# Expert second product by columns for the ranks of 144 to 176 rows, and turned back one expert later

## The chip, the cores and the metric

The kernel runs on one core of a Trainium2 chip. A core has five engines that run side by side and meet at semaphores: TensorE (PE: matrix products, and transposes through an identity matrix, with its weight loads shown apart as PEld), VectorE (DVE), ScalarE (ACT), GpSimd (POOL) and SyncE (SP, which issues DMAs). In this kernel the products of TensorE go to PSUM, and ScalarE and VectorE carry them from PSUM to SBUF. The metric is the device time of one execution in microseconds: 678.12 us before, the median of 3 runs (677.0 to 678.4).

## The reference, cut to what matters

A float32 transformer layer over 2 x 1024 tokens of 256 channels: attention, then a mixture of experts with 60 experts of 176 hidden units, four experts to a token, and a shared expert of 704 units.

```python
# x: layer norm of the tokens, [2048, 256]
weights, sel = top_k(softmax(x @ gate_w.T), 4)          # each token's four experts
for e in range(60):
    gu = x @ w13[e].T                                   # first product, 2 x 176 columns
    h = silu(gu[:, :176]) * gu[:, 176:]
    sparse += cw[:, e, None] * (h @ w2[e].T)            # second product, back to 256
shared = silu(x @ se_gate.T) * (x @ se_up.T) @ se_down.T * sigmoid(x @ shared_gate.T)
out = x_in + shared + sparse
```

The change concerns `h @ w2[e].T` alone.

## The kernel before, in words

Attention and routing come first. Routing scatters every token's row to a slot of each of its four experts in DRAM (`xg`), counts the tokens of each expert, and ranks the experts by that count. `CAPS` (L37) gives each rank a fixed number of rows: 6 ranks of 208, 4 of 192, 8 of 176, 10 of 160, 8 of 144 and 24 of 128. A rank with more than 128 rows is two tiles of half as many rows each (`tile_of`, L1164): 2 x 88 for 176, 2 x 80 for 160, 2 x 72 for 144. `turn_of` (L959) spreads the sizes evenly over the 60 places of the expert loop; its last five places are 176, 144, 128, 160, 128.

The expert loop (L1225) takes one place at a time. In the order in which it is written, place k does this:

- `up` (L910): the first product of place k, twelve TensorE instructions (six float32 matmuls of two instructions each) whose moving operand is xT, as wide as the rank has rows. ScalarE (L924, L926) and VectorE (L925, L927) make h in one of three buffers `hbuf`: a [128, 2, rows] tile with the hidden units on the partitions (128 in the first half, 48 and zeros in the second) and the tokens along the free axis.
- `turned` (L1177): the rows of place k+2, which came by DMA as `xe`, are turned by TensorE transposes (L1182) and copied to xT by VectorE (L1188).
- `second` (L1191) of place k-1. VectorE works out where each row goes back to (`place`, L952 and L956, into `dst`). For each tile of rows, TensorE holds that tile of h as the stationary operand, streams the 256 columns of w2 past it, twice for the two halves of the hidden units, and leaves rows x 256 in a PSUM tile `ye`. ScalarE copies both tiles to `ys` (L1207), and GpSimd scatters each tile by an indirect DMA to `yt` in DRAM (`send_back`, L933).
- Then SP issues the load of the rows of place k+4 (`rows_of`, L1172) and of the weights of place k+7 (`bring`, L984; eight buffers `w`, 624 KB each).

In this loop the order on ACT, DVE and SP is the written one (`manual_schedule`, L1211). PE and POOL are not in that list: there the planner of the framework chooses among instructions whose inputs it expects to be there, and prefers those written earlier. The PSUM pool `ps_y` has two buffers, handed out in turn to tiles tagged `ye`; a buffer is written again only when ScalarE has copied out what was in it two tiles before. `ys`, `dst` and xT have four buffers each; a buffer of `ys` or `dst` is free once the scatter that read it has landed.

Behind the loop stand a block for experts with more tokens than their rank holds (L1278; its condition is read by every engine, and here it is not entered), and then the second half of the shared expert (L863, L885), whose TensorE work runs while SP brings `yt` back (L1301) and VectorE adds it up with the routing weights (L1303). The first of these loads waits for the last scatter.

Of the kernel before, what the change touches and what calls it, by code (L numbers as in the profile page):

```python
# [8 lines left out]
F32 = mybir.dt.float32  # L9
# [7 lines left out]
P = 128  # L17
B, T, C = 2, 1024, 256
# [4 lines left out]
CC = C // P  # L23
# [7 lines left out]
W1C = 2 * P + 64 + IB  # L31
# [4 lines left out]

CAPS = [208] * 6 + [192] * 4 + [176] * 8 + [160] * 10 + [144] * 8 + [128] * 24  # L37
CAP = max(CAPS)
SP = CAP // 2
ES = NT * P  # L40
OB = -(-(ES - min(CAPS)) // P)
# [10 lines left out]
def attention_moe_kernel(  # L52
# [15 lines left out]
    nc = tc.nc  # L68
# [3 lines left out]
    def pool(name, bufs, side="left", space=None):  # L72

        kw = {"side": side} if space is None else {"space": space}
        s = ExitStack()
        return s.enter_context(tc.tile_pool(name=name, bufs=bufs, reuse_waits="tile", **kw)), s
# [7 lines left out]
    ident = const.tile([P, P], F32, name="ident")  # L84
# [72 lines left out]

    void = pj.tile([SP, 2, XR], F32, name="void", bufs=1)
    nc.gpsimd.memset(void, 0.0)
    nc.gpsimd.memset(void[:, :, TOK : TOK + 1], NONE)  # L160
    for e in range(E):
        rows = xg[e * ES : e * ES + CAP, :].rearrange("(t p) c -> p t c", p=SP)
        nc.sync.dma_start(rows, void)
    zero = pj.tile([P, 2, C], F32, name="zero", bufs=1)
    nc.gpsimd.memset(zero, 0.0)
    for i in range(TOPK * NT // 2):
        rows = yt[2 * i * P : 2 * (i + 1) * P, :].rearrange("(t p) c -> p t c", p=P)
# [7 lines left out]
    down = const.tile([E, E], F32, name="down")  # L175
# [47 lines left out]
    start = const.tile([P, E], F32, name="start")  # L223
# [313 lines left out]
    def scores(b, qb, jp, jj, s):  # L537
        t0, s0 = qb * QB, s * P
        scs = []
        for half in range(2):  # L540
            sc = ps_sc.tile([P, 2, QB], F32, tag="sc", name="sc")
            scs.append(sc)
            for gg in range(2):
                r = 32 * (2 * half + gg)
                nc.tensor.matmul(  # L545
                    sc[:, gg, :],
                    lhsT=kT[b][r : r + 32, jj, s0 : s0 + P],
                    rhs=qT[b][r : r + 32, jp, t0 : t0 + QB],
                    start=True,
                    stop=True,  # L550
                )
        es = []
        exps.clear()
        i = b * TPB + s
        for sc in scs:


            ex = att.tile([P, 2, QB], F32, tag="ex", bufs=4, name="ex")
            exps.append(
                nc.scalar.activation(ex, sc, AF.Exp, scale=rqk[:, 1, i : i + 1] if b == 0 else 1.0)  # L560
            )
            es.append(ex)
        return es
# [367 lines left out]
    def send_back(y, at):  # L931

        s = nc.gpsimd.indirect_dma_start(  # L933
            out=yt[:, :],
            out_offset=bass.IndirectOffsetOnAxis(ap=at, axis=0),
            in_=y,
            in_offset=None,
            bounds_check=TOPK * NT * P - 1,
            oob_is_err=False,
        )  # L940

        if scattered:
            tc.declare_no_dep(s.ins, group="back", reason="rows of their own")
        tc.add_to_no_dep_group("back", s.ins)
        scattered.append(s)

    def place(dst, rows, me):

        n = rows.shape[0]
        k0 = small.tile([n, 1], F32, tag="k0", name="k0")  # L950
        hit = small.tile([n, TOPK], F32, tag="wh", name="wh")
        nc.vector.scalar_tensor_tensor(  # L952
            hit, rows[:, SLT : SLT + TOPK], me, kplace[0:n, :], ALU.is_equal, ALU.mult,
            accum_out=k0,
        )
        nc.vector.tensor_add(dst, k0, rows[:, TOK : TOK + 1])  # L956
# [12 lines left out]
    def expert_at(r):  # L969

        if r not in nos:
            nos[r] = nc.values_load(
                byrank[0:1, r : r + 1],
                engines=(mybir.EngineType.SP,),
                min_val=0,
# [4 lines left out]
    def bring(k):  # L980

        no = expert_at(turn_of[k])
        w = wpool.tile([P, CC * W1C + 2 * C], F32, tag="w", name=f"w{k}")
        nc.sync.dma_start(w, wexp[bass.ds(no, 1)].rearrange("o p c -> p (o c)"))  # L984
        ws.append(w)
# [10 lines left out]
    with tc.manual_schedule(engines={mybir.EngineType.PE}), ExitStack() as both:  # L996
# [34 lines left out]
        ahead = scores(*order[0])  # L1031
        for r, (b, qb, jp, jj, s) in enumerate(order):
# [22 lines left out]
            if r + 1 < R:  # L1055
                ahead = scores(*order[r + 1])
# [10 lines left out]
            for g in range(NKV):  # L1067
                nc.tensor.matmul(  # L1068
                    av[32 * g : 32 * g + 32, :],
                    lhsT=vaug[:, b * TPB + s, g, H * jj : H * jj + 32],  # L1070
                    rhs=es[g // 2][:, g % 2, :],
                    start=s == 0,
                    stop=s == TPB - 1,
# [33 lines left out]
        h = RB // 2  # L1107
# [21 lines left out]
        sp_s = ExitStack()  # L1129
        sp_s.enter_context(tc.manual_schedule(engines={mybir.EngineType.SP}))  # L1130
        blocks = range(NT * P // FB)
# [23 lines left out]
        eh, eh_s = pool("eh", 1, "right")  # L1155
        hbuf = [eh.tile([P, 2, CAP], F32, name=f"hbuf{i}") for i in range(3)]
        for h in hbuf:
            nc.gpsimd.memset(h, 0.0)
        ew, ew_s = pool("ework", 4, "right")
        ps_x, ps_x_s = pool("ps_x", 2, space=PSUM)  # L1160
        ps_gu, ps_gu_s = pool("ps_gu", 2, space=PSUM)
        ps_y, ps_y_s = pool("ps_y", 2, space=PSUM)

        def tile_of(cap):  # L1164

            return (cap // 2, 2) if cap > P else (cap, 1)

        def rows_of(r):
            rows, n = tile_of(CAPS[r])
            no = expert_at(r)  # L1170
            xe = ew.tile([P, 2, XR], F32, tag="xe", bufs=XA + 3, name=f"xe{r}")[0:rows, 0:n, :]
            nc.sync.dma_start(  # L1172
                xe, xg[bass.ds(no * ES, CAPS[r]), :].rearrange("(t p) c -> p t c", p=rows)
            )
            return xe

        def turned(r, xe):  # L1177
            rows, n = tile_of(CAPS[r])
            tp = ps_x.tile([P, CC, CAP], F32, tag="tpe", name=f"tpe{r}")[:, :, 0 : CAPS[r]]
            for t in range(n):  # L1180
                for c in range(CC):
                    nc.tensor.transpose(  # L1182
                        tp[:, c, t * rows : (t + 1) * rows],
                        xe[:, t, c * P : (c + 1) * P],
                        ident[0:rows, 0:rows],
                    )
            xT = ew.tile([P, CC, CAP], F32, tag="xT", name=f"xT{r}")[:, :, 0 : CAPS[r]]
            nc.vector.tensor_copy(xT, tp)  # L1188
            return xT

        def second(r, w, h, xe):  # L1191
            rows, n = tile_of(CAPS[r])
            dst = ew.tile([P, 2], I32, tag="dst", name=f"dst{r}")[0:rows, :]
            for t in range(n):
                place(dst[:, t : t + 1], xe[:, t, :], slotid[0:rows, r, t : t + 1])
            po = ps_y.tile([P, 2, C], F32, tag="ye", name=f"ye{r}")[0:rows, 0:n, :]
            ys = ew.tile([P, 2, C], F32, tag="ys", name=f"ys{r}")[0:rows, 0:n, :]
            for t in range(n):
                for k in range(2):
                    nc.tensor.matmul(  # L1200
                        po[:, t, :],
                        lhsT=h[:, k, t * rows : (t + 1) * rows],
                        rhs=w[:, CC * W1C + k * C : CC * W1C + (k + 1) * C],
                        start=k == 0,
                        stop=k == 1,
                    )
            nc.scalar.copy(ys, po)  # L1207
            for t in range(n):
                send_back(ys[:, t, :], dst[:, t : t + 1])

        with tc.manual_schedule(  # L1211
            engines={mybir.EngineType.Activation, mybir.EngineType.DVE, mybir.EngineType.SP}
        ):
            xes = {}
            xTs = {}

            for k in range(XA):
                xes[k] = rows_of(turn_of[k])
            with tc.issue_after(added[-1].ins):
                xTs[0] = turned(turn_of[0], xes[0])  # L1220
            xTs[1] = turned(turn_of[1], xes[1])


            ahead = None
            for k, r in enumerate(turn_of):  # L1225
                h = hbuf[k % 3]
                up(xTs.pop(k), ws[k], h, CAPS[r], ps_gu, f"{r}")
                last = (r, ws[k], h, xes.pop(k))
                if k + 2 < E:
                    xTs[k + 2] = turned(turn_of[k + 2], xes[k + 2])  # L1230
                if ahead is not None:
                    second(*ahead)
                ahead = last

                if k + XA < E:
                    xes[k + XA] = rows_of(turn_of[k + XA])
                if 1 <= k and WA + k - 1 < E:
                    bring(WA + k - 1)
            second(*ahead)


    def over_block(e, j, c0, w):
# [35 lines left out]
    with tc.If(most > 0):  # L1278
        with tc.For_i(0, E) as e:
            n_e = nc.values_load(nblk[0:1, bass.ds(e, 1)], min_val=0, max_val=OB)  # L1280
            with tc.If(n_e > 0):
                w = wpool.tile([P, CC * W1C + 2 * C], F32, tag="w", name="w_o")
                nc.sync.dma_start(w, wexp[bass.ds(e, 1)].rearrange("o p c -> p (o c)"))
                c0 = nc.values_load(
                    cap0[0:1, bass.ds(e, 1)], min_val=min(CAPS), max_val=CAP
                )
# [106 lines left out]
```

## Time and profile before

| | |
|---|---|
| median of 3 runs | 678.12 us (677.0 to 678.4) |
| the profiled execution | 678.74 us |
| its span, first to last instruction | 676.9 us |
| TensorE busy, granted clock | 663.9 us (98%), 1.00 |
| before the expert loop | 0 to 419 us |
| expert loop on TensorE | 419 to about 613.2 us |
| shared expert's second half, output | 614.5 to 676.9 us |
| VectorE, ScalarE, GpSimd in 419 to 614 us | 88.8, 65.0 and 90.5 us busy of 195 |

The span is the profiled execution from its first to its last instruction; 1.8 us of its time lie outside. Busy times of TensorE are of pipelined instructions: one that is recorded as 379 ns long may be followed by the next after 216 ns, so what an instruction costs on a full TensorE is read from the starts of a row of them, not from its duration. A group "x8" of a timeline is eight instructions in a row, and eight times their spacing is the distance from its start to the start of the next group.

### The profile page before, as it was taken

What the parts mean: (1) busy time and instruction counts of PE and PEld (TensorE: products, weight loads), DVE (VectorE), ACT (ScalarE), POOL (GpSimd) and SP (SyncE); (2) the same over time, 40 slices, a digit from 0 to 9 for tenths busy, and PEclk for the clock granted to TensorE, in tenths of its full rate; (3) what the DMA queues carried; (4) which work ended last, traced back from release to release, by engine and by line L of the source; (5) the groups of instructions that cost most, each with busy time, mean ns of one, the idle gap of its engine ahead of it and who ended that gap; (6) DMA issues with size and microseconds to landing.
All of it is one profiled execution on the core that took longest, in us unless ns stands there. A gap on an engine that the chain in (4) does not pass through costs nothing. (4 is left out here: it accounts for less than half of the span.)

```text
span 676.9 us, 12425 instructions
## 1 busy us (share of the span) xinstructions
PE 663.9 (98%) x4156; PEld 375.9 (56%) x4157; DVE 361.7 (53%) x1404; ACT 355.7 (53%) x503; POOL 185.7 (27%) x250
## 2 busy tenths in 40 slices
PE   8999999999999999999999998999999999999997
PEld 7432332442224223233235477898998989885466
DVE  5653755427154376556657755444444434543984
ACT  3678778768986787877862400333333333332210
POOL 4020020011000034533135451444444454543000
PEclk9999999999999999999999999999999999999999
DMA  8999930002100011211011084799989899933951
GB/s 274 294 285 298 333 124 1 1 1 92 42 1 1 0 43 42 75 51 50 9 51 66 34 317 163 252 292 296 298 284 307 286 287 293 299 90 113 309 178 48
DMA packets 64275, 106.33 MB, mean 157 GB/s; under 512 B 7417, under 2 KB 51209, under 8 KB 64210
## 3 DMA queue, kind: packets, MB, share of 16 engines
q1 hardware_dynamic: 55010, 86.57, 39.6%
q0 software_dynamic: 7680, 17.32, 7.4%
q10 hardware_dynamic: 1520, 1.64, 0.7%
q8 instruction: 33, 0.54, 0.3%
q14 instruction: 32, 0.26, 0.1%
HBM read 64.13 MB, written 42.45 MB: 157 GB/s over the span
## 5 line engine op out<-in xcount | busy, mean ns | idle before, releaser
L545 PE MATMUL sc<-qT,kT 32*128 32x512 f32 x1024 | 160.3, 639 | 0.8 <-DVE vaug L335 0.5
L560 ACT ACTIVATE ex<-sc,rqk 128x1024 f32<-128x1024 f32 x128 | 134.2, 1111 | 36.8 <-PE sc L545 35.1
L1068 PE MATMUL av<-ex,vaug 128*32 128x512 f32 x1024 | 137.3, 604 | 2.6 <-DVE den L586 1.8
L560 ACT ACTIVATE ex<-sc 128x1024 f32<-128x1024 f32 x128 | 124.1, 1022 | 28.2 <-PE sc L545 24.6
L933 POOL DMA_INDIRECT yt<-ys,dst x96 | 92.8, 966 | 115.2 <-ACT ys L1207 67.5
L545 PEld LDWEIGHTS sc<-qT,kT 32*128 32x128 f32 x1024 | 52.7, 183 | 109.1 <-issue 67.5
L1200 PE MATMUL ye<-w,hbuf 128*128 128x256 f32 (+5 forms) x384 | 93.3, 381 | 0.0
L739 POOL DMA_INDIRECT xg<-xs,idx x64 | 63.3, 989 | 100.7 <-DVE idx L734 73.5
L863 PE MATMUL sg<-x2T,ws_sb 128*128 128x512 f32 x176 | 78.1, 596 | 1.2 <-ACTq L1278 1.2
L917 PE MATMUL gua<-xT,w 128*128 128x128 f32 (+5 forms) x480 | 73.2, 295 | 0.5 <-DVE xT L1188 0.5
L917 PEld LDWEIGHTS gua<-xT,w 128*128 128x128 f32 x480 | 70.1, 191 | 4.8 <-issue 0.6
L1207 ACT COPY ys<-ye 128x256 f32<-128x256 f32 (+5 forms) x60 | 29.9, 499 | 73.0 <-PE ye L1200 47.4
L1200 PEld LDWEIGHTS ye<-w,hbuf 128*128 128x128 f32 (+5 forms) x384 | 58.9, 164 | 14.5
L1068 PEld LDWEIGHTS av<-ex,vaug 128*32 128x32 f32 x1024 | 20.4, 107 | 79.0 <-issue 66.1
L925 DVE TENSOR_TENSOR hbuf<-hbuf,gua 128x128 f32<-128x128 f32 (+5 forms) x60 | 18.9, 315 | 85.0 <-ACT hbuf L924 45.9
L863 PEld LDWEIGHTS sg<-x2T,ws_sb 128*128 128x128 f32 x176 | 32.6, 190 | 38.9 <-issue 35.5
L924 ACT ACTIVATE hbuf<-gua 128x128 f32<-128x128 f32 (+5 forms) x60 | 17.9, 299 | 64.7 <-PE gua L917 41.8
L506 POOL TENSOR_TENSOR t<-u,rope_sb 128x128 f32<-128x128 f32 x24 | 12.4, 545 | 129.5 <-DVE u L492 129.5
L873 ACT ACTIVATE hs<-sg 128x512 f32<-128x512 f32 (+1 forms) x24 | 14.3, 596 | 59.0 <-PE sg L863 56.7
L885 PE MATMUL so<-ws_sb,hs 128*128 128x256 f32 x192 | 42.5, 381 | 1.5 <-DVE acc L893 1.5
L917 PE MATMUL gub<-xT,w 128*112 128x128 f32 (+5 forms) x240 | 41.2, 294 | 0.0
L885 PEld LDWEIGHTS so<-ws_sb,hs 128*128 128x128 f32 x192 | 36.2, 190 | 8.2 <-DVE acc L893 2.2
(184 smaller groups left out, 663.1 us busy)
## 6 DMA issues: line engine op xcount, KB each, us to landing
w<-in_wexp_dram SPq DMA_DIRECT2D x60, 624.0 KB
xg<-void SPq DMA_DIRECT2D x60, 221.0 KB
yt<-zero SPq DMA_DIRECT2D x32, 256.0 KB
got<-yt SPq DMA_DIRECT2D x16, 512.0 KB
xe<-xg SPq DMA_DIRECT2D x24, 136.0 KB
xe<-xg SPq DMA_DIRECT2D x10, 170.0 KB
yt<-ys,dst POOLq DMA_INDIRECT x96
xe<-xg SPq DMA_DIRECT2D x8, 187.0 KB
```

What stands on the lines that cost most here:

```text
L545: nc.tensor.matmul(sc[:, gg, :], lhsT=kT[b][r : r + 32, jj, s0 : s0 + P], rhs=qT[b][r : r + 32, jp, t0 : t0 + QB], start=True, stop=True,)
L560: nc.scalar.activation(ex, sc, AF.Exp, scale=rqk[:, 1, i : i + 1] if b == 0 else 1.0)
L739: s = nc.gpsimd.indirect_dma_start(out=xg[:, :], out_offset=bass.IndirectOffsetOnAxis(ap=at_, axis=0), in_=xs[:, i, :], in_offset=None, bo ...
L863: nc.tensor.matmul(p, lhsT=ws1_sb[:, c, c0 : c0 + P], rhs=x2T[:, c, n * FB : (n + 1) * FB], start=c == 0, stop=c == CC - 1,)
L885: nc.tensor.matmul(po, lhsT=hs[:, m, t * P : (t + 1) * P], rhs=ws2_sb[:, m, :], start=m == 0, stop=m == NC2 - 1,)
L917: nc.tensor.matmul(ps[part][0:m, 0:n], lhsT=w[:, c * W1C + c0 : c * W1C + c0 + m], rhs=xT[:, c, 0:n], start=c == 0, stop=c == CC - 1,)
L924: nc.scalar.activation(h[:, 0, 0:n], ps["ga"][:, 0:n], AF.Silu)
L925: nc.vector.tensor_mul(h[:, 0, 0:n], h[:, 0, 0:n], ps["ua"][:, 0:n])
L933: s = nc.gpsimd.indirect_dma_start(out=yt[:, :], out_offset=bass.IndirectOffsetOnAxis(ap=at, axis=0), in_=y, in_offset=None, bounds_check= ...
L1068: nc.tensor.matmul(av[32 * g : 32 * g + 32, :], lhsT=vaug[:, b * TPB + s, g, H * jj : H * jj + 32], rhs=es[g // 2][:, g % 2, :], start=s == 0,
L1200: nc.tensor.matmul(po[:, t, :], lhsT=h[:, k, t * rows : (t + 1) * rows], rhs=w[:, CC * W1C + k * C : CC * W1C + (k + 1) * C], start=k == 0 ...
L1207: nc.scalar.copy(ys, po)
```

## The change

For the 26 ranks of 144, 160 and 176 rows the second product is made the other way round. The stationary operand is a 128 x 128 block of w2, the moving operand is h with only as many columns as the rank has rows, and the product comes out as columns: 128 channels on the partitions, the tokens along the free axis, two such blocks in one `ye` tile. ScalarE copies that to a new SBUF tile `yT` (two buffers). One expert later, behind the next expert's second product, TensorE turns the four blocks of `yT` back to rows with transposes against the identity into another tile tagged `ye`, ScalarE copies that to `ys`, and the two scatters follow. The ranks of 208, 192 and 128 rows stay as they were.

```diff
+BY_COLUMNS = 176
@@ def second(r, w, h, xe):
-            po = ps_y.tile([P, 2, C], F32, tag="ye", name=f"ye{r}")[0:rows, 0:n, :]
-            ys = ew.tile([P, 2, C], F32, tag="ys", name=f"ys{r}")[0:rows, 0:n, :]
-            for t in range(n):
+            po = ps_y.tile([P, 2, C], F32, tag="ye", name=f"ye{r}")
+            down = w[:, CC * W1C :].rearrange("p (k c) -> p k c", k=2)
+
+            def send(po):
+                ys = ew.tile([P, 2, C], F32, tag="ys", name=f"ys{r}")[0:rows, 0:n, :]
+                nc.scalar.copy(ys, po[0:rows, 0:n, :])
+                for t in range(n):
+                    send_back(ys[:, t, :], dst[:, t : t + 1])
+
+            if not P < CAPS[r] <= BY_COLUMNS:
...
+                send(po)
+                return None
+            for c in range(CC):
                 for k in range(2):
                     nc.tensor.matmul(
-                        po[:, t, :],
-                        lhsT=h[:, k, t * rows : (t + 1) * rows],
-                        rhs=w[:, CC * W1C + k * C : CC * W1C + (k + 1) * C],
+                        po[:, c, 0 : CAPS[r]],
+                        lhsT=down[:, k, c * P : (c + 1) * P],
+                        rhs=h[:, k, 0 : CAPS[r]],
                         start=k == 0,
                         stop=k == 1,
                     )
-            nc.scalar.copy(ys, po)
-            for t in range(n):
-                send_back(ys[:, t, :], dst[:, t : t + 1])
+            yT = ew.tile([P, CC, CAP], F32, tag="yT", bufs=2, name=f"yT{r}")[:, :, 0 : CAPS[r]]
+            nc.scalar.copy(yT, po[:, :, 0 : CAPS[r]])
+
+            def turn():
+                tp = ps_y.tile([P, 2, C], F32, tag="ye", name=f"yr{r}")
+                for t in range(n):
+                    for c in range(CC):
+                        nc.tensor.transpose(
+                            tp[0:rows, t, c * P : (c + 1) * P],
+                            yT[:, c, t * rows : (t + 1) * rows],
+                            ident,
+                        )
+                send(tp)
+
+            return turn
@@ the expert loop
-            ahead = None
+            ahead = left = None
...
+                turn, left = left, None
                 if ahead is not None:
-                    second(*ahead)
+                    left = second(*ahead)
+                if turn is not None:
+                    turn()
...
-            second(*ahead)
+            for turn in (left, second(*ahead)):
+                if turn is not None:
+                    turn()
```

More of the change, by code (lines that the diff above doesn't have):

```diff
@@ L1195, in second @@
                 place(dst[:, t : t + 1], xe[:, t, :], slotid[0:rows, r, t : t + 1])
-            po = ps_y.tile([P, 2, C], F32, tag="ye", name=f"ye{r}")[0:rows, 0:n, :]
-            ys = ew.tile([P, 2, C], F32, tag="ys", name=f"ys{r}")[0:rows, 0:n, :]
-            for t in range(n):
+            po = ps_y.tile([P, 2, C], F32, tag="ye", name=f"ye{r}")
[7 more added lines that the diff above has]
+                for t in range(n):
+                    for k in range(2):
+                        nc.tensor.matmul(
+                            po[0:rows, t, :],
+                            lhsT=h[:, k, t * rows : (t + 1) * rows],
+                            rhs=down[:, k, :],
+                            start=k == 0,
+                            stop=k == 1,
+                        )
+                send(po)
+                return None
+            for c in range(CC):
                 for k in range(2):
                     nc.tensor.matmul(
-                        po[:, t, :],
-                        lhsT=h[:, k, t * rows : (t + 1) * rows],
-                        rhs=w[:, CC * W1C + k * C : CC * W1C + (k + 1) * C],
+                        po[:, c, 0 : CAPS[r]],
+                        lhsT=down[:, k, c * P : (c + 1) * P],
+                        rhs=h[:, k, 0 : CAPS[r]],
                         start=k == 0,
@@ L1206, in second @@
                     )
-            nc.scalar.copy(ys, po)
-            for t in range(n):
-                send_back(ys[:, t, :], dst[:, t : t + 1])
+            yT = ew.tile([P, CC, CAP], F32, tag="yT", bufs=2, name=f"yT{r}")[:, :, 0 : CAPS[r]]
+            nc.scalar.copy(yT, po[:, :, 0 : CAPS[r]])
+            def turn():
+                tp = ps_y.tile([P, 2, C], F32, tag="ye", name=f"yr{r}")
+                for t in range(n):
+                    for c in range(CC):
[3 more added lines that the diff above has]
+                            ident,
+                        )
+                send(tp)
+            return turn
         with tc.manual_schedule(
```

## The prediction

> **What bounds the kernel now.** I read the page first: its first part, then its chain.
>
> ```profile
> PE 663.9 (98%) x4156; PEld 375.9 (56%) x4157; DVE 361.7 (53%) x1404; ACT 355.7 (53%) x503; POOL 185.7 (27%) x250
> ...
> PE sg L863 6%; PE so L885 3%; DVE acc L893 0%
> ```
>
> The chain that ended last is TensorE alone, and it goes back only to 614.5 us, where TensorE waited for the end of the expert block. The change lies before that, so the stage has to be read for itself: busy time in a window cut inside the expert loop.
>
> ```profile
> 430.00:590.00 160.00, 160.00 (x1064) 144.00 (x1063) 73.34 (x387) 53.37 (x148) 76.89 (x80) 1.00 0.91 293
> ```
>
> In order: length, PE, PEld, DVE, ACT, POOL, clock, DMA share, GB/s. TensorE has no gap in 160 us, VectorE is busy 46%, ScalarE 33%, GpSimd 48%. DMA is the only rival, at 0.91. In the waits of the stage (419 to 614 us) TensorE's own idle time before the matmuls comes to about 1 us. So a TensorE nanosecond saved in this loop is one saved in the end, as long as DMA and the buffers keep up.
>
> Its price comes from the starts in the timeline of TensorE.
>
> ```profile
> 500.07 0.76 PE L917 MATMUL gub<-xT,w 128*112 128x176 f32 x4
> 500.67 0.38 PE L1182 MATMUL tpe<-ident,xe 128*128 128x128 f32 x2
> 500.89 1.89 PE L1200 MATMUL ye<-w,hbuf 128*104 128x256 f32 x8
> 502.62 1.14 PE L917 MATMUL gua<-xT,w 128*128 128x144 f32 x8
> 503.60 0.65 PE L917 MATMUL gub<-xT,w 128*112 128x144 f32 x4
> 504.09 0.44 PE L1182 MATMUL tpe<-ident,xe 80*128 80x80 f32 x4
> 504.37 1.90 PE L1200 MATMUL ye<-w,hbuf 128*88 128x256 f32 x8
> 506.10 1.05 PE L917 MATMUL gua<-xT,w 128*128 128x128 f32 x8
> ...
> 507.43 0.38 PE L1182 MATMUL tpe<-ident,xe 128*128 128x128 f32 x2
> 507.65 1.89 PE L1200 MATMUL ye<-w,hbuf 128*72 128x256 f32 x8
> 509.37 1.25 PE L917 MATMUL gua<-xT,w 128*128 128x160 f32 x8
> 510.46 0.71 PE L917 MATMUL gub<-xT,w 128*112 128x160 f32 x4
> ```
>
> Start to start, a float32 instruction with 256 moving columns takes (506.10 - 504.37) / 8 = 0.216 us, the same for 104, 88 or 72 stationary columns: half-filled weights save nothing, which is what the change is after. 176 columns take 0.60 / 4 = 0.150, 160 take 1.09 / 8 = 0.136, 144 take 0.98 / 8 = 0.1225. A transpose of 128 columns takes 0.22 / 2 = 0.11, and it is one instruction where a matmul is two.
>
> **What the Trainium skill says.** "Perfetto Trace Analysis", section "Identifying the Most-Contended Engine", says that matmul busy time is no measure of how full TensorE is, and to look at LDWEIGHTS busy time. Here that is 144 of 160 us, 90%, so both agree. "TensorE: Matmul & The Clock Gate", section "LDWEIGHTS (loading the stationary operand)", has a load take its stationary columns divided by 1.2 in ns: an estimate of 107 ns for 128. The trace fits: `gua` with 128 stationary and 128 moving columns runs at 0.89 / 8 = 0.111 us (506.10 to the `gub` group at 506.99), while 144 moving columns, at 0.1225, show nothing of the load. The full blocks that the change loads therefore stay hidden behind 144 columns or more. The same page, section "Part 4: PE-mode transpose", warns of about 275 ns for a transpose in context and of a copy behind it; the records do say 273 ns, but the spacing of 0.11 us is what a full TensorE pays. "Perfetto Trace Analysis", section "DMA Instruction — SWDGE (GPSIMD)", says that a scatter's record ends with its descriptors, not its data; so I took landings from the trace's semaphore records.
>
> **The change part by part, on TensorE.** Removed per expert: eight instructions x 0.216 = 1.73 us. Added: two column blocks x two halves x two instructions = eight at the rank's own width, and four transposes x 0.11 = 0.44.
> - 176 rows: 8 x 0.150 + 0.44 = 1.64, saves 0.09; eight such ranks, 0.7 us.
> - 160 rows: 8 x 0.136 + 0.44 = 1.53, saves 0.20; ten ranks, 2.0 us.
> - 144 rows: 8 x 0.1225 + 0.44 = 1.42, saves 0.31; eight ranks, 2.5 us.
>
> The sum is 5.2 us. No transpose against the full identity with 88, 80 or 72 stationary columns is in the trace; from below its cost is 0.11 (the stream), from above 0.15 if the narrow float32 load showed, which would take 26 x 4 x 0.04 = 4.2 us back. I take 0.11, since existing transposes with 128 stationary columns run at that. Each turn adds waits to TensorE's queue; the existing sixty of L917 (51 ns each) leave no gap in the starts, so nothing, and 26 x 0.05 = 1.3 us if none hides. A gain beyond 5.2 has no source in the loop but the rounding of these rows, 0.2 us.
>
> **ScalarE.** Added: 26 copies of 2 x rows elements. Between the copies of 256 (373 ns) and 512 elements (582 ns) that is 0.45, 0.425 and 0.40 us: 8 x 0.45 + 10 x 0.425 + 8 x 0.40 = 11 us on 65 of 195. It hides under TensorE. The silu of the next expert queues behind both copies, and VectorE's product behind that. The cover is the distance between h finished and h used: for the expert whose L927 ends at 605.65 us, `second` starts at 608.44, 2.8 us later.
>
> **PSUM buffers.** Two `ye` tiles per expert instead of one, in two buffers. By the written order the buffer of a product held the tile two back, which is copied before `up` and `turned` (1.6 us or more) are through; the turn's buffer likewise. `yT` is copied a whole expert (about 3.2 us) before its turn. No wait.
>
> **Scatters, `ys` and `dst`.** 52 scatters start one expert later. Queued on GpSimd behind the next expert's, they can bunch to four in a row, at 0.97 + 0.30 us each. The reuse of `dst` comes nearest:
>
> ```profile
> L956 DVEq EVENT_SEMAPHORE  x56: 21/50/50, 436.8 to 611.9; - x56
> L1207 ACT COPY ys<-ye x60: 372/581/586, 423.8 to 613.7; 128x256 f32<-128x256 f32 x24, 80x512 f32<-80x512 f32 x10, 88x512 f32<-88x512 f32 x8, 72x512 f32<-72x512 f32 x8
> ```
>
> At most 50 ns: this wait is free now. Setting the scatters' landings (2.1 to 6.5 us after their issue) against the `dst` that reuses the buffer four experts on, I find 1.3 to 9.4 us to spare, mostly 5 to 8; `ys` has 2.6 us or more. Less 3.2 us for the column ranks, about four places fall to zero or to -2 us, more with bunching. VectorE then waits a microsecond or two; behind it queue the next expert's two products and xT copy. VectorE idles 106 of 195 us, 1.8 per expert, and h has its 2.8: TensorE stands still only when a wait passes about 4.5 us. I count nothing.
>
> **SP and DMA.** No DMA is added. SP's weight load waits for the end of the product that frees `w`, which comes earlier. The same bytes in 2.7% less time ask for 0.93 of the engines instead of 0.91; weights land 13 to 16 us ahead of use almost throughout, rows 4 to 7. Nothing.
>
> **The end of the loop.** The place before the last has 160 rows, so its turn comes last: the copy that TensorE's next stage waits for is 0.58 instead of 0.37 us, plus 0.2. The last three scatters may all come behind the block at L1278, landing about 1.3 us later. The gathers then start later; VectorE there is up to 1.3 us late already, and with two buffers per product TensorE feels it from about 4 us. Nothing.
>
> **Sum.** -5.2 + 0.2 + 0.1 for the waits = -4.9 us. The profiled execution of 678.74 us (span 676.9) becomes 673.8 (672.0). It was 0.6 above the median, so against that: 678.12 - 4.9 = 673.2 us.
>
> **Rivals.** *Half of it is eaten* (gain 1.5 to 4, 674.1 to 676.6): narrow transposes at 0.15 us, visible queue waits, or DMA near its limit delaying rows. For it speaks the DMA share of 0.91; against it, that TensorE never waited for a row or weight in 160 us. *DMA takes over*, no measurable change: if 293 GB/s were all that this mix of packets can get, the loop would keep its length, 678 us; slices at 319 and 341 GB/s in the same window speak against. *TensorE waits for the turn*, slower: PE's order is not written by hand here, and if the planner set each turn behind its own product, TensorE would stand about 0.2 + 0.43 + 0.2 us for the copy each time. That is 26 x 0.83 = 21.6 less 4.9: about 695 us. It decides from a wait of 0.19 us a turn, where 26 of them are the gain. Against it: TensorE followed the written order in every expert of the trace before, and the planner takes what is ready first. That the change does not do what it says I exclude: the shapes are in the diff.
>
> **Chances.** The forecast 0.73 (own range 672.2 to 674.2), half eaten 0.11, DMA takes over 0.05, slower by the turn or a like wait 0.11. About 0.2% (1.4 us) is what a measurement of this kernel can tell from no change. So faster 0.84, same 0.05, slower 0.11. The range 671.8 to 676.8 takes in the first two and a spread of 0.1% between runs.
>
> **What would show it.** Right: inside the loop TensorE still without gaps; product rows at 128 x 176, 160 and 144 spaced 0.150, 0.136 and 0.1225; turns spaced 0.11; the shared half starting near 609.6 us. ScalarE's busy time up by 11 us. Wrong: idle time before the turn, released by ScalarE; `dst` waits of over 4 us on DVE's queue with TensorE idle behind them; turns spaced over 0.13.

## The result, and the profile after

The changed kernel took 672.55 us (median of 4 runs, 671.39 to 672.97) against 678.26 us before (677.0 to 678.5): a ratio of 0.9915, 95% interval 0.9900 to 0.9929. Forecast were 673.2 us and a range of 671.8 to 676.8. The experiments show that this holds on some chips and not on others. First comes what the profile says.

The page after, its first part and its chain:

```profile
PE 658.8 (98%) x4260; PEld 383.2 (57%) x4261; DVE 361.6 (54%) x1404; ACT 367.1 (55%) x529; POOL 185.9 (28%) x250
...
PE sg L864 6%; PE so L886 3%; DVE acc L894 0%
```

TensorE has 104 instructions more and is busy for 5.1 us less; ScalarE is busy for 11.4 us more. The chain is still TensorE's and starts behind the loop, so the loop is read for itself again: first busy time in the same window, then TensorE's timeline where a product by columns and a turn stand.

```profile
430.00:590.00 160.00, 160.00 (x1175) 153.19 (x1175) 75.20 (x393) 64.16 (x172) 80.42 (x84) 1.00 0.94 300
```

```profile
500.49 1.40 PE L1223 MATMUL ye<-hbuf,w 128*128 128x176 f32 x8
501.73 1.05 PE L918 MATMUL gua<-xT,w 128*128 128x128 f32 x8
502.62 0.60 PE L918 MATMUL gub<-xT,w 128*112 128x128 f32 x4
503.06 0.38 PE L1183 MATMUL tpe<-ident,xe 128*128 128x128 f32 x2
503.28 1.15 PE L1223 MATMUL ye<-hbuf,w 128*128 128x144 f32 x8
504.26 0.60 PE L1237 MATMUL yr<-ident,yT 128*88 128x128 f32 x4
504.69 0.57 PE L918 MATMUL gua<-xT,w 128*128 128x160 f32 x3
```

TensorE still has no gap in 160 us, with weight loads at 96% and DMA at 0.94. From starts: eight column products of 176 take 501.73 - 500.49 = 1.24 us, which is 0.155 each with the step to the next group, and 0.149 among themselves. Eight of 144 take 0.98, or 0.1225 each. A turn of four takes 0.43, with 0.109 from one start to the next, although 88, 80 or 72 columns are held and not 128.

Two costs that the prediction named: the reuse of `dst` on VectorE (the line's instructions, with durations least/median/most in ns, and what its engine sat idle for), and then the copies on ScalarE.

```profile
L957 DVEq EVENT_SEMAPHORE  x56: 21/50/50, 433.8 to 605.1; - x56
...
  DMA yt<-ys,dst: 0.3, 1
```

```profile
L1231 ACT COPY yT<-ye x26: 399/426/453, 424.9 to 605.1; 128x320 f32<-128x320 f32 x10, 128x352 f32<-128x352 f32 x8, 128x288 f32<-128x288 f32 x8
```

One wait of 0.3 us for a scatter in the whole loop, and 26 copies of the predicted length.

Stage by stage, the two profiles differ by 7.3 us of span: 2.0 ahead of the loop (its first product starts at 417.02, not 419.01), 4.96 in the loop from its first product to its last instruction (194.00 to 189.04), 0.38 from there to the shared half, nothing behind. The 2.0 us are not the change's: where both kernels were profiled on one chip (below, six places ahead), the loop begins at 417.63 and 417.25. It begins at 418.4 to 419.1 us in every profile with late increments (the next part says what these are) and at 416.9 to 417.6 in every other, so these two first profiles are of two kinds, and their 7.3 us are not the change's alone.

### The profile page after: what moved, and what is told of

It is laid out like the page before. It is cut to its first block, busy times and chain, and to the rows that moved or that the text cites. A ratio compares the mean times of both kernels' runs of the same rounds, so it can differ in the third digit from the quotient of the medians.

```text
span 669.6 us, 12632 instructions
## 1 busy us (share of the span) xinstructions
PE 658.8 (98%) x4260; PEld 383.2 (57%) x4261; DVE 361.6 (54%) x1404; ACT 367.1 (55%) x529; POOL 185.9 (28%) x250
## 5 line engine op out<-in xcount | busy, mean ns | idle before, releaser
L918 PEld LDWEIGHTS gua<-xT,w 128*128 128x128 f32 x480 | 67.5, 191 | 1.7 <-issue 0.5
L1212 PE MATMUL ye<-w,hbuf 128*128 128x256 f32 (+2 forms) x176 | 44.3, 383 | 0.0
L1205 ACT COPY ys<-ye 128x256 f32<-128x256 f32 (+2 forms) x34 | 14.8, 435 | 38.0 <-PE ye L1212 38.0
L918 PEld LDWEIGHTS gub<-xT,w 128*112 128x112 f32 x240 | 34.2, 177 | 0.0
```

The lines of the kernel that those rows point to most:

```text
L918: nc.tensor.matmul(ps[part][0:m, 0:n], lhsT=w[:, c * W1C + c0 : c * W1C + c0 + m], rhs=xT[:, c, 0:n], start=c == 0, stop=c == CC - 1,)
L1205: nc.scalar.copy(ys, po[0:rows, 0:n, :])
L1212: nc.tensor.matmul(po[0:rows, t, :], lhsT=h[:, k, t * rows : (t + 1) * rows], rhs=down[:, k, :], start=k == 0, stop=k == 1,)
```

## The experiments

Three things are worked out for every profile. *TensorE's own pace:* the spacings fit 0.833 ns per moving column plus 2.5 ns, and 0.11 us for 128 columns; what the starts exceed this by, summed over the loop, is its **excess**, and most of it is waiting where it is large. *The changed work itself:* for each of the 26 ranks, the time from the first start of its second product to the next start behind it, and its turn where it has one; their sum is **second**. *Late increments:* TensorE tells the other engines that a product is done by raising a semaphore by one. For each matmul in 420 to 612 us that does so, the time is taken from its recorded end to the next recorded update of that semaphore; the increment is **late** if this is over 0.3 us (the ends are modelled, but where none is late all lie at 0.014 us).

| kernel | chip | late / all | loop us | excess | second |
|---|---|---|---|---|---|
| before (first profile) | not told | 106/258 | 194.00 | 1.50 | 44.96 |
| before again | 3 | 97/257 | 195.63 | 3.12 | 44.95 |
| before, rows six ahead | 14 | 0/259 | 193.73 | 1.23 | 44.96 |
| after (first profile) | not told | 0/286 | 189.04 | 1.70 | 40.04 |
| after again | 3 | 114/282 | 198.07 | 10.72 | 40.10 |
| after, third | 14 | 0/286 | 191.18 | 3.83 | 40.04 |
| after, rows six ahead | 14 | 0/286 | 189.01 | 1.67 | 40.04 |
| the same, third | 0 | 115/287 | 190.78 | 3.45 | 40.11 |
| last rank by rows | 12 | 114/286 | 189.65 | 2.24 | 40.28 |
| 144 alone | 3 | 101/266 | 195.50 | 5.47 | 42.53 |
| turn at once | 3 | 88/265 | 209.25 | 22.00 | 60.38, with 26 waits in it |

The third column marks a kind of profile more than it counts: the traces with late increments also lack records of updates (after again has 645 for TensorE's 692 increments of the whole run, and 879 for VectorE's 1,020; the others lack almost none). That the signals are late shows without these records. From the recorded end of a product to the start of the ScalarE or VectorE instruction that takes it up, no step is over 0.5 us in any profile without late increments. In the others there are 43 of 238 (before), 47 of 238 (before again), 61 of 246 (144 alone), 18 of 264 (turn at once), 101 and 90 of 264 (after again; rows six ahead, third) and 88 of 263 (last rank by rows). ScalarE's signals do not share this: where VectorE is free, its product starts within 0.034 us of the end of ScalarE's silu, in every profile.

### Both kernels again, the turn without its delay, one size alone (chip 3)

Both kernels unchanged:

> The kernel before, unchanged. In its first profile TensorE reached the expert loop at 419.0 us, in the profile of the changed kernel at 417.0, with the same instructions ahead of it; VectorE had stood 3.7 us before the third sum behind the shared expert's first half, with the releaser given as remote. Theory (chance): that wait comes and goes from run to run; the loop starts anywhere from 416.8 to 419, and the loop itself takes 194.2 us again. Rival (systematic): the wait is part of the kernel before, and the loop starts at 419.0 within 0.3 us.

> The changed kernel, unchanged, for a narrower interval. Theory (TensorE's time in the loop, 5.1 us by the two profiles, and 0.3 us at its end): ratio 0.9920, 5.4 us. Rival (the 2 us ahead of the loop belong to the change as well): 7.3 us, ratio 0.9892.

The turn behind its own product instead of one expert later:

```diff
-                turn, left = left, None
                 if ahead is not None:
-                    left = second(*ahead)
-                if turn is not None:
-                    turn()
+                    turn = second(*ahead)
+                    if turn is not None:
+                        turn()
```

> The turn behind its own product instead of one expert later. Theory: TensorE then stands for the copy each time, 0.2 + 0.43 + 0.2 us, 26 times: 21.6 us on top of the changed kernel, about 694 us, slower than before. Rival (the planner of TensorE's order fills the gap with the next expert's first product): 673 us, no more than 1 us above the changed kernel.

Only the eight ranks of 144 rows by columns:

```diff
-BY_COLUMNS = 176
+BY_COLUMNS = 144
```

> Columns for the eight ranks of 144 rows alone. Theory (terms of the sum add up): 2.5 us less than the kernel before, 675.7 us, ratio 0.9963. Rival (the gain comes from something the pieces share, such as the scatters that start later or the weights that come free sooner): in proportion to the ranks, 8 of 26, 1.7 us or less, ratio 0.9975.

| | us (median) | ratio to before, 95% |
|---|---|---|
| before, beside | 678.95 (19 runs) | |
| before again | 680.16 (1 run) | |
| after again | 682.63 (6 runs) | 1.0052 (1.0037 to 1.0068) |
| turn at once | 693.63 (4 runs) | 1.0213 (1.0197 to 1.0229) |
| 144 alone | 679.52 (12 runs) | 1.0003 (0.9995 to 1.0012) |

**Before again** began its loop at 418.60 us, outside the 0.3 us of the rival, and took 195.63 us for it and not 194.2, because of two waits for rows.

**Turn at once** did as forecast. TensorE's waits in the loop:

```profile
PE yr L1237 <- ACT yT L1231: 8.9, 15, 0.9
PE yr L1237 <- issue: 6.3, 11, 0.8
```

All 26 turns wait; by the starts they lose 19.5 us, 0.75 each, where the rival had 0.83. In the changed kernel TensorE kept the written order, so the rival was never in play, but its price was right.

**After again** is the surprise: slower than before by 0.5%, with the code that had been faster. The last column of the first table shows that second products and turns took 4.85 us less here as well, and in 144 alone 2.4 us less. What came in was waiting: 10.7 us of excess against 3.1 in before again. TensorE's waits in the loop of after again:

```profile
PE tpe L1183 <- issue: 2.2, 3, 1.2
PE tpe L1183 <- DMA xe<-xg: 2.1, 3, 1.6
PE yr L1237 <- ACT yT L1231: 2.1, 1, 2.1
```

By the starts, six waits in front of the transposes of rows make 5.35 us, the last turn 2.29, and two second products whose h came late 0.82; before again has two waits for rows, 1.74. Why the rows are late is to be read on SyncE. Its waits in the loop, first of after (first profile), then of after again:

```profile
SPq L985 <- PE ye L1212: 40.0, 29, 4.0
SPq L985 <- PE ye L1223: 25.1, 22, 1.7
```

```profile
SPq L985 <- PE tpe L1183: 22.4, 7, 4.0
SPq L985 <- PE ye L1212: 15.9, 9, 5.4
SPq L985 <- PE ye L1223: 14.2, 12, 3.3
SPq L985 <- PE gub L918: 5.8, 4, 2.4
```

The weight load (L985) waits for the second product that frees its buffer, and for nothing else. In the first list it is let go by exactly these products. In the second it is let go in 11 cases by `tpe` or `gub`, which free no weights: there the product was done before, and its signal came later. One place of it, TensorE, ScalarE and SyncE:

```profile
462.76 0.87 PE L918 MATMUL gub<-xT,w 128*112 128x208 f32 x4
463.47 0.38 PE L1183 MATMUL tpe<-ident,xe 128*128 128x128 f32 x2
463.68 1.03 PE L1212 MATMUL ye<-w,hbuf 128*128 128x256 f32 x4
```

```profile
464.43 0.34 ACT L925 ACTIVATE hbuf<-gua 128x208 f32<-128x208 f32 x1 [2.30 <-PE ye L1212]
...
467.46 0.37 ACT L1205 COPY ys<-ye 128x256 f32<-128x256 f32 x1 [1.95 <-PE tpe L1183]
```

```profile
467.41 0.34 SPq L985 DMA_DIRECT2D w<-in_wexp_dram  x1
468.34 0.33 SPq L1173 DMA_DIRECT2D xe<-xg  x1
```

The matmuls of `ye` end at 463.68 + 1.03 = 464.71, but their copy starts at 467.46 and the weight load that they free goes out at 467.41: 2.7 us late, together. The silu of `gua`, whose matmuls had ended by 462.93, starts at 464.43. The rows behind that weight load on SyncE's queue are asked for at 468.34, 4.9 us ahead of their use where the kernel before has 7.2 at the median, and TensorE stands for them at 473.2 (0.49 us by the starts).

Of the six waits for rows, one more (1.75 us, at 557.0) is of this kind, behind a weight load 2.8 us late. The other four, 3.11 us together, are not: these rows were asked for 7.2 to 9.0 us ahead, as early as ever, and took 6.3 to 7.7 us from the ask to their last packet, where the median is 4.6 here and 4.7 in after (6.1 at most). The last of them, on SyncE and on TensorE:

```profile
505.95 0.34 SPq L985 DMA_DIRECT2D w<-in_wexp_dram  x1
507.72 0.34 SPq L985 DMA_DIRECT2D w<-in_wexp_dram  x1
510.43 0.34 SPq L985 DMA_DIRECT2D w<-in_wexp_dram  x1
511.38 0.00 SPq L1173 DMA_DIRECT2D xe<-xg  x1
520.40 0.47 PE L1183 MATMUL tpe<-ident,xe 72*128 72x72 f32 x4 [1.20 <-issue]
```

The first weight load is 1.2 us late behind its product, the next two 0.5 and 0.03, so three of 624 KB go out within 4.5 us; in after the same three take 5.7. The two waits at 489 and 492 us stand behind such a bunch as well (4.3 us against 5.8). So a late signal can delay rows in two ways: through the ask, or through a crowd of loads in the DMA queues. The second way is read from these times and was not tested by itself.

From the rows' last packet to their use there were 2.5 us at the median in after (least 1.1) and 1.9 in after again (least 0.6). Where TensorE stood for rows, this step took 0.6 to 1.3 us in after again and up to 2.4 in other profiles, so little of the 2.5 is to spare.

**144 alone** met neither number. Its second products and turns took 2.4 us less, and 5.47 us of excess ate it: between the other two, as are its late hand-overs. Seven waits make 3.65 us of it, three for rows (1.80) and four in front of second products (1.85).

The shared half behind the loop was longer, too: 65.3 us in after again, 62.35 in every other profile of the two kernels. The slice of the granted clock on its page has an 8:

```profile
PEclk9999999999999999999999999999999999998999
```

From 616.70 us on TensorE ran at half clock for 6.83 us. Just before, it had stood 2.1 us for the last turn; another 0.9 us, for the next block, fell into the slow stretch itself:

```profile
612.62 1.39 PE L1212 MATMUL ye<-w,hbuf 128*128 128x256 f32 x4
616.14 0.63 PE L1237 MATMUL yr<-ident,yT 128*80 128x128 f32 x4 [2.12 <-ACT yT L1231]
617.65 1.22 PE L864 MATMUL sg<-x2T,ws_sb 128*128 128x512 f32 x1 [0.89 <-ACTq L1318]
```

The Trainium skill, "TensorE: Matmul & The Clock Gate", section "Part 1: The HAM clock gate (the "warmup" mystery)", has the clock go to half after an idle window of about 3.4 us, on a free-running grid. 6.83 us is two such windows; but in the 3.4 us before the drop TensorE was idle for 2.1 and not for all, so here less than a whole idle window went with it. All six runs of after again had a clock of 0.994 or 0.997. The others on chip 3, which have no turn behind the last product, had 0.999 or 1.0, all 12 of 144 alone and all four of turn at once among them. That speaks for the last turn as what the clock fell on.

So the difference of the two profiles on chip 3, +4.8 us of span, is: second products and turns -4.85, the rest of the loop (waits) +7.3, the clock +2.9, the step at the end of the loop -0.4, the start -0.2. Of the waits, 3.6 us are for rows and 2.3 for the last turn. Rows are thus about a third of the 10.2 us that came in, and the last turn with the clock is half.

**The theory then:** some chips hand on TensorE's increments late; this delays SyncE, which asks late for the rows, whose slack is small. **Rivals:** DMA itself is at its limit; the increments cost through h, PSUM and the last turn rather than through the rows; or that job was an odd one.

### The chip, and the rows asked for earlier (chip 14)

The changed kernel once more, and both kernels with two more places of lead for the rows (nine `xe` buffers instead of seven):

```diff
-XA = 4
+XA = 6
```

and the changed kernel without most weight loads, so that most experts multiply by another's weights:

```diff
+        if k >= WA:
+            ws.append(ws[k - WA])
+            return
         no = expert_at(turn_of[k])
```

> The changed kernel once more, to see whether its time goes by the load and the chip. In the profile of the changed kernel that came with the result (672.55 us) none of TensorE's 286 recorded semaphore increments in the expert loop reached its recorded update over 0.3 us after the instruction's end; in the repeat on another day (682.63 us) 114 of 282 did, and in the kernel before 106 of 258. Theory (the loss comes with late increments: they hold up SyncE, which then asks for the rows late): if under 10 of them are late, 671 to 674 us; if some 100 are late, 680 to 684 us and 6 to 11 us of waits of TensorE in the loop. Rival (the repeat was an odd one): some 100 late and still 671 to 675 us.

> The changed kernel with the rows of an expert asked for six places ahead, not four, so that SyncE may be two experts (6.3 us) late with them. Theory: where increments come late, the waits in front of the transposes of rows (6.2 us in six of them in the profile of 682.9 us span) go, and with them the half-clock stretch behind the loop mostly: 674 to 677 us, against 680 to 684 of the changed kernel in the same job; where increments come on time, within 1 us of the changed kernel, 672 to 673.5. Rival (DMA at its limit delays the rows themselves): the same waits, time within 1.5 us of the changed kernel. Rival (late increments cost through other waits, of h, PSUM or the turn): under 2 us gained.

> The kernel before with the same six places, as the control. Theory: it had 1.5 to 3.1 us over TensorE's own pace in the loop, two waits for rows of 1.7 us in one profile and none in the other, so it gains 0 to 2 us: ratio 0.997 to 1.000; and the change is then worth 4 to 6 us at six places, on any chip. Rival (six places help both alike because DMA works more evenly): it gains as much as the changed kernel does.

> The changed kernel without the weight loads of the places from the ninth on: those places use the weights of the place eight before, so their output is not the product with their own weights. It takes 52 x 624 KB from the loop. Theory (TensorE's increments come late because the completions of so many DMA packets crowd the semaphores): under 15 of some 280 late, no waits for rows, loop 187 to 189 us, 671 to 674 us. Rival (they are late for a cause in the chip or the load that has nothing to do with DMA): 80 to 120 late as in the changed kernel of the same job, if that has them. If that one has none, this run tells nothing on it.

(The 6.2 us of row waits in the second text should read 5.35.)

| | us (median) | ratio to before, 95% |
|---|---|---|
| before, beside | 677.01 (15 runs) | |
| after, third | 671.76 (4 runs) | 0.9920 (0.9904 to 0.9937) |
| after, rows six ahead | 671.65 (4 runs) | 0.9920 (0.9904 to 0.9937) |
| before, rows six ahead | 676.90 (12 runs) | 0.9993 (0.9984 to 1.0002) |
| after without weight loads | 671.02 (1 run) | |

No increment is late on this chip, in either kernel, and the change is worth 5.25 us with and without the longer lead. The rows are tight even here: in the profile of after, third (its slowest run, 674.21 us) TensorE waits for them, and with six places it does not (slack 6.7 us at the least).

```profile
PE tpe L1183 <- DMA xe<-xg: 2.0, 3, 1.5
```

Without 52 of the 60 weight loads the loop takes 189.01 us, as with them at six places: with that lead, crowded DMA costs nothing here. With four places it did, in after, third: no signal was late and the rows were asked for 7.7 and 8.6 us ahead, but they took 6.2 us to their last packet, where the median is 4.5, and 2.0 without the weight loads. So the rival of DMA at its limit has a part. On late increments that run says nothing, as its text foresaw.

### A chip with late increments again

Rows six ahead was run twice more, to meet such a chip:

> The changed kernel with the rows asked for six places ahead, once more, for a chip whose increments come late. If some 100 of 286 increments of TensorE come over 0.3 us late, as on chip 3: theory (late increments hold up SyncE and so the rows) 674 to 677 us, waits in front of the transposes of rows under 1 us in sum, ratio to the kernel before 0.994 to 0.998, where the changed kernel had 1.005 on chip 3; rival (late increments cost through h, the turn and the half clock behind the loop) 680 to 683 us, ratio 1.002 to 1.006. If under 10 are late, as on chip 14: 671.65 us again, and nothing is told apart.

Chip 4: none late, 671.75 us, before 677.79, ratio 0.9908 (0.9891 to 0.9924).

> The same kernel, changed and with the rows asked for six places ahead, on whatever chip comes, since chips 14 and 4 had no late increments. On a chip with some 100 late increments of 286: theory (they hold up SyncE and so the rows) ratio to the kernel before 0.994 to 0.998 and under 1 us of waits in front of the transposes of rows; rival (they cost through h, the turn and the half clock) ratio 1.002 to 1.006, as the changed kernel on chip 3. On a chip with under 10 late: 671 to 672.5 us, and only the share of such chips is learned.

Chip 0: 115 of 287 late. 678.11 us (16 runs, 675.93 to 680.43) against 679.30: ratio 0.9977 (0.9962 to 0.9992). TensorE's waits from 417 to 608 us:

```profile
PE gua L918 <- DVE xT L1189: 0.5, 1, 0.5
PE yr L1237 <- ACT yT L1231: 0.4, 1, 0.4
```

As many late increments as on chip 3, late hand-overs as well (90 against 101), and no wait for rows, with rows that took up to 7.2 us to their last packet. The ratio lies in the theory's range. The changed kernel with four places was not run on this chip, so what the lead is worth is read across two chips. The rival of other waits has a part as well. Seven of the 16 runs had a clock of 1.0, and took 675.93 to 676.73 us (median 676.27); nine had 0.994 to 0.997, and 677.63 to 680.43 (median 679.61). In the profile, of a run at 1.0, the last turn waits 1.15 us by the starts. It has one product of 0.86 us to hide the copy that it waits for, since no first product follows it.

So the last rank by columns (place 58, 160 rows) was made as before:

```diff
-XA = 4
+XA = 6
...
-            if not P < CAPS[r] <= BY_COLUMNS:
+            if not P < CAPS[r] <= BY_COLUMNS or r == turn_of[E - 2]:
```

> Changed, rows asked for six places ahead, and the last rank by columns (place 58, 160 rows) made as before, so that no turn stands at the end of the loop with only one product of 0.86 us as its cover. On a chip with some 100 late increments: theory (the last turn waits 1.2 to 2.3 us there for a late copy, TensorE then stands again for the next block, and the clock is halved for one or two windows behind it, as in nine of the sixteen executions on chip 0): clock 1.00 or 0.999 in every execution, 675.5 to 677 us, ratio to the kernel before 0.994 to 0.997, where it was 0.9977 with the last turn. Rival (the half clock comes from waits all over the loop): clock 0.994 to 0.997 in half of the executions again, ratio 0.997 to 0.999. On a chip with under 10 late: 671.5 to 672.2 us, the turn saved (0.44 us) against the product at the rows' price (0.64 us) and the longer last copy; nothing told apart.

Chip 12: 114 of 286 late. 676.00 us (5 runs) against 679.21: ratio 0.9959 (0.9945 to 0.9973). Four runs had 1.0 and took 675.68 to 676.53; one had 0.997 and took 677.65. So one run in five had half clock for a while where the theory said none, against nine in sixteen with the last turn. With so few runs, on different chips and with intervals of the ratio that overlap, this does not show what leaving out the last turn is worth; that it does not end the half clock altogether is shown. In its profile TensorE still stands 2.28 us for the next block, at full clock.

The last run asked whether dense DMA is needed for late increments:

> The changed kernel without the weight loads of the places from the ninth on (those places multiply by the weights of the place eight before, so their output is another), once more, since chip 14 had no late increments with or without them. Chips 3, 0 and 12 had 114, 115 and 114 late increments of some 285, nearly all from 400 us on, where DMA is dense. On such a chip, theory (it takes dense DMA as well): under 30 late in the loop, no waits of TensorE for rows, span 669 to 672 us. Rival (they are late whatever DMA does): 80 to 120 late. On a chip like 14 and 4: none late, 669 us, and this stays open.

It came to chip 14 again: none late, 671.27 us. Open, as its text says.

## Why the prediction was right, and where it was not

The forecast holds where TensorE's signals come on time (672.55 us; 671.76 on chip 14). That the first measurement met such a case was luck: on chip 3 the same code took 682.63 us, outside the range.

**TensorE's terms: right.** Forecast -5.2 us; second products and turns took 44.96 us before and 40.04 after, -4.92, and 40.10 even on chip 3. By size: -0.59 for 176 rows (forecast 0.7), -1.91 for 160 (2.0), -2.43 for 144 (2.5), and the last is the same with 144 alone. What is missing is mostly the first step of each product by columns, which is longer than those behind it (0.177 us against 0.149 at 176 columns). The upper bound of 0.15 us for narrow turns is out; they take 0.109.

**ScalarE, PSUM, `dst`: right.** ScalarE was busy 75.7 us in the loop of 189 instead of 65.0 in 195. TensorE waited for no `ye` buffer in the profile after, and one `dst` wait took 0.3 us.

**End of the loop: wrong in sign.** Forecast +0.2 us for the longer last copy, measured -0.38 from the last TensorE start to the shared half (1.54 to 1.16). The last copy runs directly behind the one ahead of it; in the kernel before, ScalarE began it 0.36 us after the last product's end. In after again this end cost most: 2.3 us for the turn put there, and 2.9 of clock behind it.

**"SP and DMA. Nothing", with rows landing "4 to 7" us ahead: the step that failed.** The slack of the rows was 1.2 us at the least and 2.6 at the median in the very profile that the prediction used, from the packets' times; the ask stands 7.2 us ahead of the use, and 4.3 of them go for the landing. With increments on time that is enough, but for 2 us in one profile. With increments late it is not: 5.35 us of waits for rows, 3.6 more than in the kernel before beside it. Six places ahead the waits for rows are gone with just as many late increments, though on another chip.

**The rival "half of it is eaten"** named delayed rows, as a matter of DMA near its limit, and that is one half of what was found. Two of the six waits on chip 3 come from SyncE's queue (rows behind a weight load behind a late signal), and four are for rows that were asked for in time and long under way; two such waits stand in after, third with no late signal at all. Without the weight loads nothing was gained on chip 14 beyond what the lead of six places gives; on a chip with late increments that wasn't tried. The rival's price, 0.9 to 3.4 us of the gain, was too low for chip 3, where all 4.9 and 3.7 us more were lost.

**The profile used, too.** 106 of its 258 increments were late, and 43 of its 238 hand-overs from TensorE to ScalarE and VectorE took over 0.5 us; the prediction read ScalarE's cover as if TensorE's signals came at once.

**Open.** Why chips 3, 0 and 12 hand on increments late and 14 and 4 do not; every profile on the former had them, none on the latter. And why the changed kernel is hit harder: on chip 3 over 0.5 us were 47 of 238 hand-overs in before again, 61 of 246 in 144 alone, 101 of 264 in after again, but 18 of 264 in turn at once. This follows how closely TensorE is packed (turn at once has the changed kernel's instructions, but 26 pauses), yet no run varied that alone. The signals were seen only while the profiler recorded, so whether recording has a part in their lateness is not known. Neither the kernel before with six places ahead nor the changed one with four was run on chip 0 or 12, so what part of the gain there is the lead's and what the change's is not told apart.

## What to carry to other kernels

Count a saving on the bounding engine from the spacing of starts, and then check the slack of every transfer behind that engine's signals, from its last packet to its use: with some 2.5 us at the median, a gain of 5 us turned into a loss of 3.7 on another chip. Where a queue issues loads in order, ask for the small urgent ones early enough that neither a late release of a big one ahead of them nor a crowd of big ones does harm: two places more cost only buffers, and lost nothing where they were not needed (671.65 against 671.76 us). And be wary of a step at the end of a loop with little work to hide its wait: in after again the last turn's wait and the clock behind it took 5.2 us. For a chip that is not known, the version with six places ahead is the one to take; that the last rank by rows improves on it is not shown.

## What the runs showed of the hardware

- On chips 3, 0 and 12 a third to two fifths of TensorE's increments in the loop had no recorded update within 0.3 us, and engines that were free took products up to 3.6 us late, several signals then coming within 0.3 us; on chips 14 and 4 it was one increment of over 1,600, and no late hand-over. Ahead of 400 us there were ten at most. ScalarE's signals to VectorE were on time in all of them. The kernel before took 678.95 to 679.30 us (medians) on the former and 677.01 and 677.79 on the latter.
- Idle for 2.1 of 3.4 us, TensorE fell to half clock for 6.83 us, which cost 2.9 us; in the profile of last rank by rows it stood 2.28 us and kept its clock.
- A transpose holding 72, 80 or 88 columns of data and streaming the 128 of the identity has the 0.109 us spacing of one that holds 128.
